# A two-layer graph network with expert layers on one core: the second attention's maximum by TensorE, a shorter choice of experts, and the first edges' terms loaded earlier

## The chip, the cores and the metric

The kernel runs on one core of a Trainium2 chip. The metric is the device time in microseconds of one execution: the median of several runs, lower is better. The core's engines are TensorE (PE, with PEld for its weight loads), VectorE (DVE), ScalarE (ACT), GpSimd (POOL) and SyncE (SP, which issues most DMAs). A matmul on 32-bit floats shows in the profile as two passes.

## What is computed

3125 nodes with 256 features, 100000 edges sorted by their target. Four residual steps, each on a normalized copy of `x`:

```python
x = x + gat(layernorm(x), edges, ...)          # two attention layers, 4 heads and 1 head
x = x + ffn0(layernorm(x))                     # 8 experts, two chosen once for all rows
x = x + gcn(layernorm(x), edges, ...)          # a linear layer, two graph convolutions
x = x + ffn1(layernorm(x))                     # 8 experts, two chosen for each row
```

Attention over the edges into a node (with a loop at each node) is

```python
e = leaky_relu(al_s[src] + al_d[dst], 0.2)
alpha = exp(e - segment_max(e, dst)) / segment_sum(...)     # for each target node
out = segment_sum(h[src] * alpha, dst)
```

and the first expert layer chooses its two experts from the mean row:

```python
routing = softmax(mean(x, axis=rows) @ Wr + br)
load = routing * N
scale = where(load > capacity, capacity / load, 1)          # capacity = ceil(N * 1.25 / 8)
routing = softmax(routing * scale);  top 2, softmax over the two, weights for both experts
out = layernorm(sum of the two weighted experts + x)
```

## The kernel before

Rows lie in 25 blocks of 128 nodes, in five groups of five. The stages follow each other on one core, each with work of the next one slipped in as "spare" tasks.

**Edges and the first attention layer** (0 to 990 us, `FirstLayer`). A counting pipeline (`count_step`, 391 chunks of 256 edges) makes a dense matrix of edge counts by one-hot matmuls (L1778). The first three blocks of nodes are computed densely from it. The other nodes go edge by edge: 258 chunks in 65 batches of four. For each batch POOL gathers the rows of the sources (L1918, eight indirect DMAs, a ring of three batches), SP loads `edge_turn` (the targets' places, L1933) and four small `window`s (the targets' terms, 14 to 20 rows of 16 bytes, L1937, each at an address that SP reads into a register at L1584). DVE makes one-hots of `edge_turn` (`place_turn`, L1951), PE picks the terms by them (`pick_terms`, L1964), DVE and ACT make the weights (L1973, L1980, L1985), DVE spreads them (L1991), PE multiplies (L2005), DVE adds to `agg` (L2018). The self loops of a piece of nodes are put into `agg` by `new_sums`: SP loads `loop_x` and `by_node` (L2064, L2066), DVE multiplies (L2075).

In `run`, ahead of the loop, the order written is: `open_sums`, eight gathers, the tasks of `new_sums(0)` each followed by a counting step, then the windows of batches 0 and 1 (L2387 to L2389), then `place_turn(0)`, `pick_terms(0)`, and so on. The framework schedules each engine's instructions by priority and readiness as it models them; priority is the order written. In the parts before and inside the loop `in_order` fixes the order on PE, DVE and ACT as written (before it on SP too); between them it does not.

**End of the first layer, second product** (990 to 1084). `norm_terms` makes scale and shift on small tiles (its Sqrt is L918), ACT applies them with Relu (L931), PE multiplies by W2 (L937), DVE sums the two attention terms of each block into the last two columns of `h2` (L943), ACT copies `h2` (L945).

**Second attention** (1084 to 1386). `sd` is copied from `h2` (L987). `attention_columns` takes maximum and minimum of the source terms on DVE (L784, L786) and over the partitions by a reduction on POOL (L790), makes three sets of columns (L802) and the flag for a range over 60. `attend_all` then runs 125 steps. For each group it transposes the target column (L829) and makes the two halves of `ab` on ACT (L831); each step has z on DVE (L840), Exp on ACT (L842), the product with the counts on DVE (L848) and ten PE passes into `po` (L857). Spare tasks ahead of the others are `degrees` (L947) and the nine arithmetic checks on the chunks' ranges (`check_tasks`, L1492), whose result decides at the very end whether a slow general version runs again.

**First expert layer** (1386 to 1634). The spare tasks of the last group normalize it, transpose it (L1232, L1233) and sum it over its nodes (L1237). `choose` makes the mean, the logits (L1263), two softmaxes with the load correction between them (L1266 to L1279), ranks, the experts' numbers (L1292), loads W1 and W2 of both (L1298, L1301), picks their bias (L1308), makes the two shares and scales W2 by them (L1322), and makes the mixed second bias (L1330 to L1335). POOL adds it to `xa` and beta to `x` (L1356, L1357). The loop over 13 chunks of nodes has W1 (L1384), Gelu into `hid` (L1387), W2 (L1394) and the sum (L1397). The pool `route` with `choose`'s small tiles is closed before `hid` is allocated, so `hid` may lie on the same memory, and a tile's first write waits for the last reader of what lay there.

**Convolutions and second expert layer** (1634 to the end). Two layers of dense products with the counts (L1100), with the routing of the second expert layer as spare tasks, then slots of 256 rows through their experts (L2877, L2887) and scattered sums (L2892).

Of the kernel before, what the change touches and what calls it, by code (L numbers as in the profile page):

```python
# [764 lines left out]
class Fast(Kernel):  # L765
# [13 lines left out]
    def attention_columns(self, sd, n, pool, doubt):  # L779


        nc = self.nc
        ends = pool.tile([P, 2, n], F32, name="ends")
        nc.vector.tensor_reduce(ends[:, 0, :], sd[:, :, :n].rearrange("p b k -> p k b"), AX.X,  # L784
                                ALU.max)
        nc.vector.tensor_reduce(ends[:, 1, :], sd[:, :, :n].rearrange("p b k -> p k b"), AX.X,  # L786
                                ALU.min)
        nc.vector.tensor_scalar(ends[:, 1, :], ends[:, 1, :], -1.0, None, op0=ALU.mult)
        top = pool.tile([P, 2, n], F32, name="ends_all")
        nc.gpsimd.partition_all_reduce(top.rearrange("p a k -> p (a k)"),  # L790
                                       ends.rearrange("p a k -> p (a k)"), P,
                                       bass_isa.ReduceOp.max)
        gap = pool.tile([1, n], F32, name="gap")
        nc.vector.tensor_add(gap, top[0:1, 0, :], top[0:1, 1, :])
        nc.vector.tensor_scalar(gap, gap, 60.0, None, op0=ALU.is_le)
        nc.vector.tensor_reduce(doubt, gap, AX.X, ALU.min)
        nc.vector.tensor_scalar(doubt, doubt, -1.0, 1.0, op0=ALU.mult, op1=ALU.add)
        cols = pool.tile([P, n, 3, NB], F32, name="att_cols")
        for k in range(n):
            for i, (x, op, f) in enumerate(((k, ALU.subtract, 0.2), (k, ALU.subtract, 0.8),  # L800
                                            (n + k, ALU.add, 0.8))):
                nc.vector.tensor_scalar(cols[:, k, i, :], sd[:, :, x], top[:, 0, k:k + 1], f,  # L802
                                        op0=op, op1=ALU.mult)
        return cols

    def attend_all(self, units, work, psum_out, aux, spare, loose=()):
# [7 lines left out]
        rows, cnts, zs, ws, pos = {}, {}, {}, {}, {}  # L814

        def lead(t):
# [6 lines left out]
            if j == 0:  # L823
                ab = work.tile([P, 2, GW], F32, name="ab", bufs=2)
                for b0, n in ((0, 3), (3, 2)):
# [39 lines left out]
        for t in range(n):  # L865
# [10 lines left out]
            if j == NB - 1:  # L876
                for i in range(GB):
                    units[u][2](g, i, pos[i])
# [310 lines left out]
class SharedExperts:  # L1189
# [147 lines left out]
    def run(self, onward, keep):  # L1337
# [4 lines left out]
        with ExitStack() as ctx:  # L1342
# [34 lines left out]
            for c0 in range(0, NP, n):  # L1377
                c1 = min(c0 + n, NP)
                hid = work.tile([P, 8, n], F32, name="hid")
                for r in range(2):  # L1380
                    for f in range(4):
# [7 lines left out]
                        if f % 2:  # L1389
                            go_on(1)  # L1390
# [1620 lines left out]
```

## Time and profile before

| What | us |
|---|---|
| median of three runs | 2423.31 (2422.38 to 2425.56) |
| the profiled execution, its own time | 2423.23 |
| its span in the profile | 2421.4 |
| PE busy in the span | 2110.2 (87%) |
| PEld, DVE, ACT, POOL busy | 1753.4, 1295.4, 1192.5, 738.0 |
| last L937 ends, first L857 starts | 1084.13, 1102.90 |
| last L857 ends, first L1384, first L1394 | 1385.79, 1418.01, 1428.96 |

A row of the order of time has start, duration, engine, line, operation, output and inputs by their names, shapes, and a count of instructions that were merged. In brackets stands the idle time of the engine ahead of it and what ended it; "remote" is a semaphore that the profile can't name, "issue" is time in which nothing that the profile shows was waited for. Times in the text that no row shows (a DMA's landing, one instruction of a merged row) are from the same execution's records. The granted clock of PE is either full (1.0) or half (0.5) at any time.

### The profile page before, as it was taken

How to read it: one execution, taken by the hardware profiler on the slowest of the kernel's cores; microseconds unless marked ns; L12 is line 12 of the kernel's file. 1: busy time of each engine (PE TensorE's matmuls, PEld its weight loads, DVE VectorE, ACT ScalarE, POOL GpSimd, SP SyncE). 2: the span in 40 equal slices, each digit the busy share in tenths (PEclk: the TensorE clock that was granted, in tenths of full speed). 3: DMA queues.
4: the chain of work that ended last, by engine and by line, in shares of the span. 5: the costliest groups of instructions: out<-in, count | busy, mean ns of one | idle time of the engine just before them, and what ended most of it. 6: DMA issues, size and time to landing. Idle time of an engine off the chain costs nothing. (4 is left out here: it accounts for less than half of the span.)

```text
span 2421.4 us, 35452 instructions
## 1 busy us (share of the span) xinstructions
PE 2110.2 (87%) x10573; PEld 1753.4 (72%) x10573; DVE 1295.4 (53%) x4225; ACT 1192.5 (49%) x2785; POOL 738.0 (30%) x749
## 2 busy tenths in 40 slices
PE   5477688797988888898999969999999998999997
PEld 5366566575666666777888758887887777888886
DVE  7667556575666666327888844334335765112221
ACT  3267666666777765623445425445434444222221
POOL 1666466666566771200000050000000323222221
PEclk9977899999999988898999979999999999999998
DMA  7433455465465665896222010003324546666773
GB/s 230 136 99 97 125 158 151 134 188 163 139 182 177 206 183 164 285 332 217 68 71 80 28 39 1 1 23 114 123 82 152 198 149 216 185 179 204 233 203 80
DMA packets 232172, 350.84 MB, mean 145 GB/s; under 512 B 38358, under 2 KB 175305, under 8 KB 228257
## 3 DMA queue, kind: packets, MB, share of 16 engines
q1 hardware_dynamic: 193697, 261.00, 33.4%
q0 software_dynamic: 36608, 86.14, 13.8%
q8 instruction: 88, 1.44, 0.2%
q10 hardware_dynamic: 1664, 1.31, 0.2%
q14 instruction: 115, 0.94, 0.1%
HBM read 262.68 MB, written 86.19 MB: 144 GB/s over the span
## 5 line engine op out<-in xcount | busy, mean ns | idle before, releaser
L1918 POOL DMA_INDIRECT edge_rows<-table,pick x516 | 524.3, 1016 | 318.3 <-PE edge_sums L2005 120.1
L2005 PE MATMUL edge_sums<-edge_moves,edge_rows 128*128 128x120 f32 x2064 | 319.0, 303 | 15.5 <-issue 9.0
L2005 PEld LDWEIGHTS edge_sums<-edge_moves,edge_rows 128*128 128x128 f32 x2064 | 298.8, 216 | 44.2 <-issue 14.0
L1100 PE MATMUL po<-parts,cnt_r 128*128 128x512 f32 x1250 | 312.0, 402 | 4.3 <-ACT cnt_r L1094 2.6
L1778 PE MATMUL ps<-hot_key,hot_lo 128*128 128x350 f16 (+2 forms) x782 | 203.3, 355 | 104.2 <-DVE acc L1808 28.3
L1800 ACT CAST acc<-ps 128x325 f32 (+2 forms) x391 | 179.2, 458 | 222.1 <-PE ps L1778 64.2
L857 PE MATMUL po<-h,w 128*128 128x257 f32 x1250 | 276.7, 382 | 3.3 <-ACT o L1006 2.3
L1100 PEld LDWEIGHTS po<-parts,cnt_r 128*128 128x128 f32 x1250 | 232.3, 189 | 54.9 <-ACT cnt_r L1094 3.4
L857 PEld LDWEIGHTS po<-h,w 128*128 128x128 f32 x1250 | 236.8, 191 | 38.9 <-ACT o L1006 3.9
L2879 ACT ACTIVATE hid<-ph,ffn_b 128x256 f32<-128x256 f32 (+1 forms) x232 | 105.9, 457 | 273.6 <-PE ph L2877 253.3
L1764 ACT ACTIVATE hot_lo<-iota_key,lo 128x128 f16<-128x128 f16 x662 | 229.0, 398 | 0.0
L1758 DVE TENSOR_SCALAR hot_key<-iota_key,key 128x350 f16<-128x350 f16 (+2 forms) x782 | 225.7, 326 | 1.2 <-issue 1.2
L2877 PE MATMUL ph<-xe,ffn_w 128*128 128x256 f32 (+1 forms) x928 | 195.4, 366 | 10.0 <-DVE o L1115 5.9
L1778 PEld LDWEIGHTS <-hot_lo 128*128 128x128 f16 x782 | 81.2, 110 | 155.9 <-issue 92.0
L2887 PE MATMUL py<-ffn_w,hid 128*128 128x256 f32 x848 | 190.1, 382 | 0.0
L2877 PEld LDWEIGHTS ph<-xe,ffn_w 128*128 128x128 f32 x928 | 163.7, 193 | 33.7 <-remote 6.3
L2887 PEld LDWEIGHTS py<-ffn_w,hid 128*128 128x128 f32 x848 | 160.5, 192 | 20.9
L2892 POOL DMA_INDIRECT out<-y,to x53 | 82.7, 1560 | 305.0 <-DVE y L2891 161.2
L842 ACT ACTIVATE z<-z,att_cols 128x640 f32<-128x640 f32 x125 | 103.2, 830 | 145.3 <-DVE z L840 121.1
L2018 DVE TENSOR_TENSOR agg<-agg,edge_sums 128x180 f32 (+1 forms) x258 | 80.3, 311 | 161.8 <-PE edge_sums L2005 49.3
L2251 PE MATMUL po<-x_rows,w 128*128 128x256 f32 x600 | 156.9, 398 | 5.6 <-issue 3.7
L1808 DVE TENSOR_TENSOR acc<-acc,ps 128x25 f32 x391 | 101.4, 259 | 87.1 <-ACT acc L1800 44.2
(448 smaller groups left out, 3235.6 us busy)
## 6 DMA issues: line engine op xcount, KB each, us to landing
ffn_w<-in_L_ffn_W SPq DMA_DIRECT2D x58, 1024.0 KB
cnt_h<-cnt SPq DMA_DIRECT2D x50, 800.0 KB
rows<-blank SPq DMA_DIRECT2D x109, 258.0 KB
cnt<-cnt SPq DMA_DIRECT2D x25, 800.0 KB
cnt<-acc SPq DMA_DIRECT2D x45, 400.0 KB
first_out<-first SPq DMA_DIRECT2D x56, 192.0 KB
normed<-first_out SPq DMA_DIRECT2D x16, 640.0 KB
cnt<-cnt SPq DMA_DIRECT2D x20, 480.0 KB
```

What stands on the lines that cost most here:

```text
L857: nc.tensor.matmul(pos[i][:, :D + 1], lhsT=w[:, ts(i, P)], rhs=moving[:, j, :D + 1], start=(j == 0), stop=(j == NB - 1))
L1100: nc.tensor.matmul(pos[b], lhsT=c[:, j - j0, ts(b, P)], rhs=parts[i][:, j].rearrange("p a m -> p (a m)"), start=(j == 0), stop=(j == NB - 1))
L1758: nc.vector.tensor_scalar(h[:, u, :NB * w], self.wide[:, :NB * w], self.key[:, t:t + 1], None, op0=ALU.is_equal)
L1764: nc.scalar.activation(l[:, u, :], self.wide[:, :P], AF.Abs, bias=self.lo[:, t:t + 1], scale=-1.0)
L1778: last = self.nc.tensor.matmul(ps[:, :n], lhsT=l[:, u, :], rhs=h[:, u, :n], start=(u == 0), stop=(u == CT - 1))
L1800: ins = self.nc.scalar.copy(self.acc[g][:, :, ds(o + 1, width(c) - 1)], self.parts[c][:, :, 1:])
L1918: return self.nc.gpsimd.indirect_dma_start(out=self.ring[:, e % (RB * BT), :], out_offset=None, in_=self.table, in_offset=bass.IndirectOff ...
L2005: nc.tensor.matmul(ps[:, f * 4 * w:f * 4 * w + EW], lhsT=self.rows_of(m)[:, e, ts(f, P)], rhs=self.spread[m % 2][:, e * 5 * w:e * 5 * w + EW],
L2251: self.nc.tensor.matmul(self.pos[i], lhsT=w[:, ts(i, P)], rhs=self.k.x[:, j, :], start=(j == 0 and i % 2 == 0), stop=(j == NB - 1), skip_g ...
L2877: nc.tensor.matmul(ph, lhsT=w1[:, c, ts(f, P)], rhs=xe[:, c, :], start=(c == 0), stop=(c == 1))
L2879: nc.scalar.activation(hid[:, f, :], ph, AF.Gelu, bias=b1[:, f:f + 1])
L2887: nc.tensor.matmul(py, lhsT=hid[:, f, ts(i, P)], rhs=w2[:, f, :], start=(f == 0), stop=(f == NF - 1))
```

## The change

Five things are changed.

1. The windows of batch 0 are written ahead of the first gathers and of `new_sums(0)`; those of batch 1 stay where they were.
2. `attention_columns` becomes `attention_top`: DVE's maximum, a transpose on PE, DVE's maximum along the row, and two matmuls with a row of +1 and of -1 that put the maximum and its negative on all partitions. Two sets of columns instead of three; the third goes into the bias of the Relus that make `ab`, and Exp's scale becomes -0.8. For the first group the target columns are transposed ahead (`spread_ends`), and one half of `ab` is made on DVE. The sums of L943 go straight into `sd`. The minimum and the flag become spare tasks (`range_tasks`), `degrees` becomes several small tasks behind eight empty ones.
3. `norm_terms` issues one Exp (with scale 0) behind its Sqrt.
4. `check_tasks` move from the second attention to the second convolution layer.
5. The first expert layer: the last group's sums are taken block by block behind each transpose. The correction `where(load > capacity, ...)` is a minimum of the routing with capacity / N; the division by N is folded into the bias's addition; ranks are taken from these values, and the second softmax is made behind the loads of the weights. The experts' numbers are picked in one instruction each. The mixed bias takes one matmul (`second_bias`), called behind the first four hidden tiles of the first chunk, and POOL's adds to `xa` and `x` follow it; those to `x` also wait for the scaled W2. `route` stays open, so `hid` lies elsewhere.

```diff
-    def attention_columns(self, sd, n, pool, doubt):
...
+    def attention_top(self, sd, signs, pool, psum):
+        nc = self.nc
+        ends = pool.tile([P, 2], F32, name="ends")
+        nc.vector.tensor_reduce(ends[:, 0:1], sd[:, :, 0], AX.X, ALU.max)
+        ps = psum.tile([P, 512], F32, name="po")
+        nc.tensor.transpose(ps[:1, :P], ends[:, 0:1], self.ident)
+        most = pool.tile([1, 1], F32, name="ends_most")
+        nc.vector.tensor_reduce(most, ps[:1, :P], AX.X, ALU.max)
+        for i in range(2):
+            nc.tensor.matmul(ps[:, P + i:P + i + 1], lhsT=signs[:, i, :], rhs=most, start=True,
+                             stop=True)
+        top = pool.tile([P, 2], F32, name="top")
+        nc.vector.tensor_copy(top, ps[:, P:P + 2])
+        cols = pool.tile([P, 2, NB], F32, name="att_cols")
+        for i, f in ((1, 1.0), (0, 0.2)):
+            nc.vector.tensor_scalar(cols[:, i, :], sd[:, :, 0], top[:, 0:1], f, op0=ALU.subtract,
+                                    op1=ALU.mult)
+        return cols, top, ends, most
...
+                top = units[u][1]
+                for b0, n, pt in units[u][2] if t == 0 else spread(units[u][3], g):
+                    part = lambda i: ab[:, i, b0 * P:(b0 + n) * P].rearrange(
+                        "p (i n) -> p i n", n=P)
+                    nc.scalar.activation(part(0), pt[:, :n, :], AF.Relu, bias=top[:, 1:2],
+                                         scale=-1.0)
+                    if t == 0:
+                        nc.vector.tensor_scalar(part(1), pt[:, :n, :], top[:, 0:1], 0.0,
+                                                op0=ALU.add, op1=ALU.max)
+                    else:
+                        nc.scalar.activation(part(1), pt[:, :n, :], AF.Relu, bias=top[:, 0:1])
...
         nc.scalar.activation(rstd, diff, AF.Sqrt, bias=self.eps)
+        nc.scalar.activation(t[0:1, 5, 0:1], diff[0:1, 0:1], AF.Exp, scale=0.0)
...
-            spare = deque([lambda: self.degrees(first, work, aux)] + first.check_tasks(work))
+            wait = lambda: None
+            spare = deque([wait] * 8 + self.degree_tasks(first, work, aux)
+                          + self.range_tasks(sd, ends, most, work, aux, self.doubt[:, 3:4]))
+            self.checks = first.check_tasks
...
+            spare.extend(self.checks(work))
             layer(1, work, finish1)
...
+        def turn_last(b):
+            turn(b)
+            n0 = (g * GB + b) * P
+            add_up(g + b, n0, n0 + P)
...
-        nc.vector.tensor_add(rw[:, 0, :], pl, br)
-        k.softmax8(rw, rw, route, "sm0", 1)
...
-        nc.vector.tensor_mul(rw, rw, load)
-        k.softmax8(rw, rw, route, "sm1", 1)
+        nc.vector.scalar_tensor_tensor(rw[:, 0, :], pl, 1.0 / N, br, op0=ALU.mult, op1=ALU.add)
+        top = route.tile([P, 1], F32, name="sm0_top")
+        nc.vector.tensor_reduce(top, rw, AX.X, ALU.max)
+        nc.vector.tensor_scalar(rw[:, 0, :], rw[:, 0, :], top, None, op0=ALU.subtract)
+        nc.scalar.activation(rw, rw, AF.Exp)
+        total = route.tile([P, 1], F32, name="sm0_total")
+        nc.vector.tensor_reduce(total, rw, AX.X, ALU.add)
+        nc.vector.reciprocal(total, total)
+        nc.vector.tensor_scalar(rw[:, 0, :], rw[:, 0, :], total, cap / N, op0=ALU.mult,
+                                op1=ALU.min)
...
+        k.softmax8(rw, rw, route, "sm1", 1)
...
+        for r in range(2):
+            self.scaled = nc.vector.tensor_scalar(self.w2[:, r], self.w2[:, r], tw[:, r:r + 1],
+                                                  None, op0=ALU.mult)
+        return own, b2
+
+    def second_bias(self, own, b2, ps_y):
+        k, nc = self.k, self.nc
+        pb = ps_y.tile([P, D], F32, name="py")
+        nc.tensor.matmul(pb, lhsT=own.to_broadcast([8, P]), rhs=b2, start=True, stop=True)
         nc.scalar.copy(self.b2, pb)
+        for b in range(NB):
+            nc.gpsimd.tensor_add(self.xa[:, b, :], self.xa[:, b, :], self.b2)
+            late = nc.gpsimd.tensor_add(k.x[:, b, :], k.x[:, b, :], self.beta)
+            self.tc.add_manual_dep(late.ins, self.scaled.ins.name, SYNC)
...
+                    if c0 == 0 and r == 0:
+                        self.second_bias(*shares, ps_y)
...
             self.open_sums(ctx, w1, stats)
+            for c in range(self.size[0]):
+                self.window(0, c)
             for e in range(BT):
                 self.gather(e)
...
-            for m in range(2):
-                for c in range(self.size[m]):
-                    self.window(m, c)
+            for c in range(self.size[1]):
+                self.window(1, c)
```

## The prediction

> **What bounds the kernel now.** I read the busy times by stage first, then the matmul queue's pauses, then the order of time inside each pause. The chain of waits is of no use here: it names only the last scatter. In the stages view the columns after each window are its length, the busy time of PE, PEld, DVE, ACT and POOL with counts, the granted clock and the DMA share.
>
> ```profile
> core 0: us, PE busy (x) PEld busy (x) DVE busy (x) ACT busy (x) POOL busy (x), PEclk, DMA share, GB/s
> 73.70:80.20 6.50, 0.00 (x0) 0.00 (x0) 2.50 (x11) 0.35 (x1) 4.90 (x5) 1.00 0.38 104
> 80.20:1084.10 1003.90, 819.42 (x4512) 656.41 (x4512) 602.14 (x2251) 638.15 (x1815) 541.08 (x551) 0.90 0.57 171
> 1084.10:1102.90 18.80, 3.10 (x14) 2.05 (x13) 12.58 (x74) 6.02 (x13) 0.52 (x2) 0.64 0.94 312
> 1102.90:1385.80 282.90, 280.58 (x1305) 244.08 (x1305) 237.32 (x389) 131.62 (x190) 0.24 (x2) 0.99 0.26 83
> 1385.80:1429.00 43.20, 16.09 (x54) 11.49 (x55) 26.01 (x88) 11.79 (x24) 28.10 (x41) 0.60 0.18 56
> 1429.00:1826.00 397.00, 391.09 (x1790) 324.62 (x1788) 148.37 (x418) 179.90 (x318) 8.61 (x19) 1.00 0.17 57
> ```
>
> PE is busy nearly all the time from 1102.9 to 1385.8 and from 1429 on. Between, it stands still three times: 6.5 us before the first edges, 18.8 us ahead of the second attention layer, 43.2 us around the choice of experts (16.1 us of work in it). Behind each pause comes work that PE sets the pace of (or, in the edge loop, queues that feed each other in a fixed order), so a pause cut by x us should move all that follows by x.
>
> **1. Terms of the first edges.** PE's own order of time, then DVE's (start, duration, engine, line, groups; in brackets the idle time and who ended it):
>
> ```profile
> 80.28 1.03 PE L1964 MATMUL edge_sums<-window,edge_turn 128*128 128x16 f32 x4 [6.59 <-remote]
> 83.11 0.35 DVE L1951 TENSOR_SCALAR edge_turn<-edge_turn,part_place 128x256 f32<-128x256 f32 x1 [4.53 <-DMA edge_turn<-places]
> ```
>
> SP issued the four window DMAs of batch 0 between 68.1 and 81.1, its register instructions between them taking 0.70 us each where they take 0.03 elsewhere, and only then (81.84) the second edge_turn. The change issues edge_turn 0, the register load (1.50) and four windows (0.45 each at SP's undisturbed pace of 90 us) when SP is free, from about 61 us: they are in by 66. What is moved behind them is SP's three pairs of loop_x and by_node, whose issue costs the same 1.2 us a pair. They go later by 1.8 us (if edge_turn and the register load fit SP's idle 59.05 to 61.09) to 3.9. The first by_node had landed 0.5 us before L2075 took it at 67.3, so that DVE line slips 1.3 to 3.4 us, and with it L1951 (74.59 before), which PE's L1964 needs: 76 to 78 instead of 80.28. The next late thing is DVE's second L1951 at 83.11, whose load now goes out near 72.5 and lands by 75; the rows of gathers 0 to 7 landed at 74.8. So L1973 comes at 79 to 80.5 instead of 83.51. POOL's gathers do not wait for SP. I take **-3.5 us**; bounds -6.6 (the whole pause) and +3 (the loads 3.4 late and SP slow all the same). 64 batches follow in the same source order, which should carry this to 990.
>
> **2. Exp's table ahead (norm_terms).** One Exp behind the Sqrt makes ACT load a table there. The first Sqrt load in the trace takes 1.28 and ACT idled 0.88 for DVE's chain, 993.15 to 994.02; load and activation (1.28 + 0.2) end at 994.67: **+0.65** on the first L931, which PE waits for. Bounds 0 (if it is put behind the first Relus) and +1.5. The gain, no load at 1098.9, is in the next sum.
>
> In the trace an activation starts 0.01 us behind its load's end (1098.90 + 1.28, then 1100.19). The Trainium skill ("ScalarE: Activation LUTs", What ACT_TABLE_LOAD costs) puts a drain of about 1.38 us behind each load; by it, as an estimate, this edit would cost about 2.0 instead of 0.65. The trace disagrees, and I stay with it.
>
> **3. The maximum by TensorE.**
>
> ```profile
> 1085.59 0.15 DVE L788 TENSOR_SCALAR ends<-ends 128x1 f32<-128x1 f32 x1
> ...
> 1094.89 0.37 POOL L790 PARTITION_ALL_REDUCE ends_all<-ends  x1 [9.56 <-DMA deg_cols<-deg_row]
> ...
> 1096.05 1.33 PE L829 MATMUL aux<-ident,att_cols 128*128 128x128 f32 x5 [11.91 <-DVE att_cols L802]
> ...
> 1098.90 1.28 ACT L842 ACT_TABLE_LOAD   x1
> 1102.90 13.48 PE L857 MATMUL po<-h,w 128*128 128x257 f32 x53 [1.02 <-DVE w L848]
> ```
>
> From the ends (1085.74) to the reduced row 9.15 us pass on POOL, then transposes, ab, z, table load, exp, w. The new chain from L943's last sum at 1084.95: max 0.18 (L784); transpose into a bank that L945 has just left at 1085.35, 0.44 to its reader (L958); reduce 0.28 (L960); two matmuls with one row, four passes like L1263, 1.05; copy 0.16: 1087.4. On DVE two columns (0.2 each) and the two halves of ab, 0.46 and 0.35: 1088.6. On ACT the other halves, 0.75; but there the gcn weights' six DMA issues (L1051 to L1059) run from 1085.04 to 1088.36 and will stand ahead: 1089.15. Then z 0.87, exp 0.83, w 0.82 with small gaps: PE at 1091.75 instead of 1102.90. The transposes of b (1.33 before) hide under the wait. Counts, needed at 1090.9, landed at 1089.0. The check arithmetic on DVE (1085.9 to 1102) is gone from here; degrees and the range test come as spare tasks beside a PE that is 99% busy. dinv's Sqrt (L1061), done in the pause before, will then cost two table loads in the loop; such a pair at 1340.65 left PE running. **-11.2 us**; bounds -12.5 (ACT's issues not ahead: -11.7, and a faster start) and -9 (K=1 matmuls and DVE's order worse than the rows).
>
> **4. The short choice.**
>
> ```profile
> 1398.88 0.65 DVE L1270 TENSOR_SCALAR load<-rw 128x8 f32<-128x8 f32 x1
> ...
> 1409.77 0.64 DVE L1288 SCALAR_TENSOR_TENSOR scr<-hot,expert 128x8 f32<-128x8 f32 x1
> ...
> 1410.45 0.63 DVE L1292 TENSOR_SCALAR number<-eid 1x2 int32<-1x2 f32 x1
> 1411.01 0.15 DVE L1308 SCALAR_TENSOR_TENSOR scr<-small,hot 128x8 f32<-128x8 f32 x1
> ...
> 1418.01 5.49 PE L1384 MATMUL ph<-xa_t,ffn_w 128*128 128x256 f32 x12 [0.46 <-ACT ffn_b_sum L1335]
> ...
> 1422.71 1.28 ACT L1387 ACT_TABLE_LOAD   x1 [4.75 <-DVE ffn_w L1322]
> ```
>
> DVE's eight-element instructions take 0.65 while POOL adds beta (1396.74 to 1413.79) and 0.15 to 0.23 otherwise or with a PSUM source. The change takes the load correction and the second softmax off the chain, and POOL's adds behind it. From ACT's last copy at 1394.03: the last block's sum 0.2 (2x106 elements; 1.33 for 2x1130), mean 0.16, PE 1.06: DVE at 1395.6 (1396.91 before). Seven steps at 0.16 to 0.26 with gaps: 1.6. Ranks, five at 0.19 to 0.26: 1.15. Two picks 0.45, number 0.14: 1398.95 instead of 1411.08. SP issues 0.70 later, and the first w1 landed 3.53 us after its issue: PE at 1403.2. It now waits for no bias, and the hidden tile no longer lies on `route`, so Gelu need not wait for the scaled w2 (4.75 before). PE: 12 passes at the half clock's 0.427, 20 at 0.216 and the bias's two: 9.9 us, so L1394 starts at 1413.1 instead of 1428.96. w2, landed 6.5 and 7.3 after issue, is scaled by 1409.9, in time; Gelu starts near 1405 at 0.47 each, faster than PE delivers. POOL's 50 adds (0.7 each) now run 1410 to 1445 beside PE; L1397 takes block b at about 1416.7 + 6.9b, POOL has it at 1410.7 + 1.4b. **-15.8 us**; bounds -17.3 and -12.1 (only the chain's part).
>
> **5. Checks moved** into the second convolution layer: about 9 us of DVE in small pieces where PE is bound and DVE is idle half the time, one more SP issue (0.25). At the seam of the layers (1816 to 1827), where PE, ACT and DVE hand on in turn, a few may be in the way: **+0.5**, bounds 0 and +2.5.
>
> Sum: -3.5 + 0.65 - 11.2 - 15.8 + 0.5 = -29.35. The profiled execution took 2423.23 us (span 2421.4), the runs' median is 2423.31, so 2423.2 - 29.3 = **2394 us**.
>
> **Rivals.**
> - The first edges gain nothing: the self loops' loads come late on a DVE that works in order, and SP stays slow. For it: L2075's loads had 0.5 us to spare. Against: PE and DVE stood 6.6 and 4.5 us for just these transfers. 2394 + 3.5 to 6.5 = 2399. Chance 0.20.
> - The choice doesn't do all it says: Gelu still ends up behind the scaled w2. Then only 12.1 of 15.8 comes: 2398. For it: the wait of 4.75 is on a tile reused in memory, and the new layout may lay `hid` on another late tile. Chance 0.12.
> - The clock stays full in the shortened pauses. Before, it was half from 1389.7 to 1423.8 and for 17.1 us from 1089.3; the first eight full-size passes behind the pause took 0.427 instead of 0.216. Both starts would gain about 1.7 and 2.6: 2390. Against: the pause of 3.15 us at 2044.5 already brought 3.4 us of half clock. Chance 0.08. The Trainium skill ("TensorE: Matmul & The Clock Gate", Part 1, and Part 4 on PE-mode transposes) says that an idle window of some 3.4 us is enough, and that transposes don't count as busy; by it the clock falls here too, as I forecast.
> - Slower: the edge loop's pace. In its static order each of 64 batches (13.3 us apart) waits for its edge_turn or rows; if windows now meet the loads of loops in SP's queue in every batch, as SP did at 92.75 to 103.9, each loses time. From 29.3/64 = 0.46 us a batch it eats all gains; at 1 us the time is 2394 + 64 = 2458. Against: source order inside the loop is unchanged. Chance of slower 0.06; of just cancelling 0.03.
> - The forecast: 0.51.
>
> The forecast alone reaches from 2388 to 2401. With the first two rivals and the unknown bounds I give 2386 to 2407. A measurement here tells 0.2% (about 5 us). Faster 0.91, same 0.03, slower 0.06.
>
> **What would show it.** PE's L1964 near 77 and L1973 near 80; the last edge sums some 3.5 us earlier; no POOL reduce at L790's place and L857's first matmul some 8 us behind the last L937; number 5 us behind the last xa_t copy, DVE at 0.2 there, L1394 some 19 us behind it; every later stage as long as before. I am wrong if the stage from the first batch to 990 changes its length by over 3 us, if SP's windows are still slow, or if Gelu again waits for ffn_w.

## The result, and the profile after

| | before | after |
|---|---|---|
| median of five runs, us | 2423.31 (2419.06 to 2429.86) | 2403.42 (2402.05 to 2410.10) |
| profiled execution, its span | 2423.23, 2421.4 | 2402.05, 2400.3 |

The ratio is 0.992, with a 95% interval of 0.990 to 0.9939: 20 us faster, where 29 were forecast. Stage by stage, from the records of the two profiled executions (the text's differences are made of these):

| Stage | before | after | difference |
|---|---|---|---|
| start to the first edge multiplication | 87.43 | 87.65 | +0.22 |
| from there to the last edge sums | 872.58 | 872.37 | -0.21 |
| to the end of the second product | 124.12 | 123.72 | -0.40 |
| to the first weighted multiplication of the second attention | 18.76 | 7.27 | -11.49 |
| second attention's loop on PE | 282.89 | 284.08 | +1.19 |
| to the last copy of xa_t | 8.25 | 8.25 | 0.00 |
| choice and first experts, to the first convolution multiplication | 243.93 | 228.71 | -15.22 |
| convolutions and second experts, to the last W1 multiplication | 762.59 | 767.68 | **+5.09** |
| sum | 2400.55 | 2379.73 | -20.82 |

The stages view after, in windows that answer to those of before (length; busy PE, PEld, DVE, ACT, POOL with counts; granted clock, DMA share, GB/s):

```profile
core 0: us, PE busy (x) PEld busy (x) DVE busy (x) ACT busy (x) POOL busy (x), PEclk, DMA share, GB/s
73.70:82.00 8.30, 0.49 (x2) 0.10 (x1) 2.90 (x6) 0.35 (x1) 3.90 (x5) 1.00 0.68 198
82.00:1083.80 1001.80, 806.79 (x4514) 648.96 (x4515) 600.42 (x2256) 640.63 (x1817) 538.45 (x554) 0.91 0.58 172
1083.80:1091.00 7.20, 1.33 (x10) 0.84 (x8) 5.43 (x17) 2.94 (x5) 0.47 (x3) 0.81 0.88 309
1091.00:1375.10 284.10, 281.74 (x1313) 244.83 (x1313) 237.42 (x391) 136.38 (x196) 0.00 (x0) 0.99 0.30 96
1375.10:1403.00 27.90, 15.33 (x52) 11.69 (x53) 15.46 (x84) 11.74 (x23) 9.11 (x12) 0.63 0.29 85
1403.00:1800.30 397.30, 391.39 (x1791) 324.70 (x1789) 149.28 (x426) 179.27 (x317) 27.63 (x47) 1.00 0.17 57
1800.30:1812.00 11.70, 9.40 (x29) 7.46 (x30) 8.93 (x50) 4.72 (x5) 0.00 (x0) 0.71 0.42 140
```

The pause of 18.8 us ahead of the attention is 7.2, the stretch around the choice is 27.9 instead of 43.2. The pause ahead of the first edges is still there, and 8.3 us long. The last row is new: a stretch at the seam of the two convolution layers with a mean granted clock of 0.71.

**The first edges after** (PE's and DVE's order of time):

```profile
79.14 1.23 DVE L2137 TENSOR_TENSOR agg<-loop_x,by_node 128x1024 f32<-128x1024 f32 x1 [2.54 <-issue]
80.58 0.25 DVE L1823 TENSOR_SCALAR hot_lo<-iota_key,lo 128x128 f16<-128x128 f16 x1 [0.20 <-issue]
81.30 1.23 DVE L2137 TENSOR_TENSOR agg<-loop_x,by_node 128x1024 f32<-128x1024 f32 x1 [0.47 <-issue]
...
82.07 1.04 PE L2026 MATMUL edge_sums<-window,edge_turn 128*128 128x16 f32 x4 [5.40 <-DVE hot_lo L1823]
...
83.14 0.19 DVE L2035 TENSOR_TENSOR edge_p<-edge_sums,edge_rows 128x32 f32<-128x32 f32 x1
```

L2026 is the old L1964, L2035 the old L1973. All four windows were on their way by 70.1. But the first pick starts at 82.07, later than before (80.28): its row names DVE's `hot_lo` (L1823, a step of the counting) as what ended the wait, and DVE has the first of the self loops' products (L2137) ahead of that. These products come at 79.14 and 81.30 instead of 67.30 and 68.75, since their rows were issued only from 73.2 on.

**The maximum and the choice after**:

```profile
1084.48 0.17 DVE L785 TENSOR_REDUCE ends<-sd 128x1 f32<-128x25 f32 x1
...
1085.02 0.27 PE L787 MATMUL po<-ident,ends 128*1 128x128 f32 x1 [0.73 <-ACT h L978]
...
1086.38 0.16 DVE L794 COPY top<-po 128x2 f32<-128x2 f32 x1 [0.76 <-PE po L791]
...
1089.22 0.83 ACT L872 ACTIVATE z<-z,att_cols 128x640 f32<-128x640 f32 x1 [1.63 <-DVE z L870]
...
1091.05 3.34 PE L887 MATMUL po<-h,w 128*128 128x257 f32 x7 [4.70 <-DVE w L878]
```

```profile
1386.25 0.23 DVE L1332 TENSOR_SCALAR rw<-rw,sm_total 128x8 f32<-128x8 f32 x1
...
1388.12 0.16 DVE L1345 TENSOR_SCALAR number<-eid 1x2 int32<-1x2 f32 x1
...
1392.21 1.19 PE L1393 MATMUL py<-ffn_b,own_share 8*128 8x256 f32 x2 [6.45 <-issue]
1393.33 9.90 PE L1444 MATMUL ph<-xa_t,ffn_w 128*128 128x256 f32 x32
1403.07 7.07 PE L1456 MATMUL py<-ffn_w,hid 128*128 128x256 f32 x32
```

From the column's maximum (1084.65) to the copy of the result (1086.54) 1.9 us pass, where 9.5 passed by POOL (1085.74 to 1095.26). DVE's eight-element steps take 0.16 to 0.23 down to the number, which is ready 4.94 us behind the last copy of xa_t (17.05 before).

**The seam of the convolution layers after** (ACT and PE), where the five microseconds begin to go:

```profile
1800.39 0.48 ACT L1122 ACTIVATE split<-aux,dinv 128x256 f32<-128x256 f32 x1 [0.79 <-PE aux L1119]
1800.76 1.78 ACT L1143 CAST cnt_r<-cnt_h 128x1920 fp32r<-128x1920 f16 x1
...
1802.60 9.69 PE L1149 MATMUL po<-parts,cnt_r 128*128 128x512 f32 x29 [2.31 <-ACT cnt_r L1143]
```

The same place before:

```profile
1825.43 1.79 ACT L1094 CAST cnt_r<-cnt_h 128x1920 fp32r<-128x1920 f16 x1
1827.13 0.47 ACT L1073 ACTIVATE split<-aux,dinv 128x256 f32<-128x256 f32 x1
...
1827.27 12.99 PE L1100 MATMUL po<-parts,cnt_r 128*128 128x512 f32 x56 [1.06 <-ACT cnt_r L1094]
```

The second layer's first multiplication waits for the counts' cast, which now stands in ACT's order behind the last block's `split` (before, ahead of it), and 2.31 us pass instead of 1.06. In the clock's records it is half from 1801.6, within that pause, to 1808.5; before, it stayed full there.

### The profile page after: what moved, and what is told of

It is laid out like the page before. It is cut to its first block, busy times and chain, and to the rows that moved or that the text cites. A ratio compares the mean times of both kernels' runs of the same rounds, so it can differ in the third digit from the quotient of the medians.

```text
span 2400.3 us, 35484 instructions
## 1 busy us (share of the span) xinstructions
PE 2100.4 (88%) x10578; PEld 1746.8 (73%) x10578; DVE 1282.4 (53%) x4222; ACT 1196.3 (50%) x2785; POOL 734.5 (31%) x751
## 5 line engine op out<-in xcount | busy, mean ns | idle before, releaser
L2067 PE MATMUL edge_sums<-edge_moves,edge_rows 128*128 128x120 f32 x2064 | 313.3, 299 | 13.1 <-issue 10.2
L1149 PE MATMUL po<-parts,cnt_r 128*128 128x512 f32 x1250 | 319.5, 409 | 5.0 <-ACT cnt_r L1143 3.8
L2067 PEld LDWEIGHTS edge_sums<-edge_moves,edge_rows 128*128 128x128 f32 x2064 | 293.1, 212 | 42.2 <-issue 17.9
L1840 PE MATMUL ps<-hot_key,hot_lo 128*128 128x350 f16 (+2 forms) x782 | 198.0, 346 | 117.7 <-DVE acc L1870 41.4
L1149 PEld LDWEIGHTS po<-parts,cnt_r 128*128 128x128 f32 x1250 | 235.2, 191 | 60.0 <-ACT cnt_r L1143 4.6
L1826 ACT ACTIVATE hot_lo<-iota_key,lo 128x128 f16<-128x128 f16 x662 | 227.6, 395 | 0.0
L2940 PE MATMUL ph<-xe,ffn_w 128*128 128x256 f32 (+1 forms) x928 | 195.0, 366 | 11.2 <-DVE o L1164 6.2
L2950 PEld LDWEIGHTS py<-ffn_w,hid 128*128 128x128 f32 x848 | 159.1, 190 | 20.5
```

Of the source, the lines that this page charges most:

```text
L1149: nc.tensor.matmul(pos[b], lhsT=c[:, j - j0, ts(b, P)], rhs=parts[i][:, j].rearrange("p a m -> p (a m)"), start=(j == 0), stop=(j == NB - 1))
L1826: nc.scalar.activation(l[:, u, :], self.wide[:, :P], AF.Abs, bias=self.lo[:, t:t + 1], scale=-1.0)
L1840: last = self.nc.tensor.matmul(ps[:, :n], lhsT=l[:, u, :], rhs=h[:, u, :n], start=(u == 0), stop=(u == CT - 1))
L2067: nc.tensor.matmul(ps[:, f * 4 * w:f * 4 * w + EW], lhsT=self.rows_of(m)[:, e, ts(f, P)], rhs=self.spread[m % 2][:, e * 5 * w:e * 5 * w + EW],
L2940: nc.tensor.matmul(ph, lhsT=w1[:, c, ts(f, P)], rhs=xe[:, c, :], start=(c == 0), stop=(c == 1))
L2950: nc.tensor.matmul(py, lhsT=hid[:, f, ts(i, P)], rhs=w2[:, f, :], start=(f == 0), stop=(f == NF - 1))
```

## Experiments

Twelve runs on three more chips, four on each. On all three the kernel before takes about 2275 us instead of 2423 (the last section comes to that). So each run is compared with a run of the changed kernel on its chip, or by stage lengths that hardly differ between chips; on the first of the three, with the runs on the tests and the first two on part 1, there is no run of the changed kernel.

**The kernels themselves.** 

> The changed kernel itself, unaltered, beside the others on one chip: the measure for all runs that differ from it by one edit. Both theories of each edit expect it 0.8% under the kernel before, as on the first chip; where the chip runs the edge loop faster, the microseconds and not the share should stay: 18 to 22 us.

> The kernel before, unaltered, for its stage lengths on the same chip as the others. If SP's and DVE's instructions take their normal time here ahead of the first batch, the waits of 6.5 us that part 1 was to shorten are shorter from the start; if they take 0.7 us until the gathers' rows are in, the first multiplication is at 87 as in the first profile.

> The changed kernel itself once more, as the measure for the three others on this chip. On the two chips so far it stood 0.8 and 1.1% under the kernel before; 0.7 to 1.2% here.

Measured: after_again 0.9893 of the kernel before (0.9869 to 0.9918; 2257.38 us), before_again 1.0008, after_third on the fourth chip 0.9917 (0.9901 to 0.9932; 2256.08). The gain stays as microseconds: 17 and 21.5. Stage lengths of the kernels with the changed order of the tests: from first convolution to last W1 753.7 to 757.6 (most 754.5) against 748.19 before; the edge loop, 743.7 to 756.1, scatters over 12 us from execution to execution and hides small edits in it. In before_again the first edge multiplication is at 78.09, in after_again at 79.19: here too part 1 gains nothing.

**Where did five microseconds go: the tests at the seam.** In one run the nine index tests are written behind the first group of the second layer, in the other among the attention's tasks:

```diff
-            spare.extend(self.checks(work))
             layer(1, work, finish1)
...
                 if b % GB == GB - 1:
                     spare.extend(router.tasks(b - GB + 1, GB, out))
+                if b == GB - 1:
+                    spare.extend(self.checks(work))
```

> The changed kernel with the first layer's nine index tests (the moved work of part 5) put behind the first group of the second convolution layer instead of ahead of it. Theory 'seam': the tests only hurt because their DVE pieces push the casts of the first counts behind them, which makes TensorE's pause between the two layers 2.31 us instead of 1.06 and lets the clock fall to half for 6.8 us right after it. Then the pause is 1.06 again, the clock stays full at the seam, the stretch from the first matmul of layer 0 to the last slot's end is some 4 us shorter than the changed kernel's 767.7 us (763 to 764.5), and the time is 2398 to 2400. Rival 'the work itself': nine tests cost their DVE time wherever they stand in this layer; then the stretch stays at 767 to 768 and the time within 2 us of the changed kernel's 2403. Second rival 'the clock falls anyway': pause 1.06 but still half clock behind it; stretch about 766.5.

> The changed kernel with the same nine index tests back among the spare tasks of the second attention loop, where they stood before the change, behind the degree and range tasks. Theory 'seam': the seam of the convolution layers is as before (pause 1.06, full clock), the stretch from layer 0 to the last slot 763 to 764.5 instead of 767.7; the attention loop, whose TensorE is 99% busy and whose DVE has 40 of 283 us free, keeps its 284.0 us within 0.5; time 2398 to 2400. Rival: the tests delay the weights of that loop, which gets 1 to 5 us longer, and the gain at the seam is lost: 2400 to 2404.

Measured: 0.9889 (0.9868 to 0.991; 2248.76 us) and 0.9899 (0.988 to 0.9918). The stretch is 748.16 and 750.15, some 6 and 4 us less; the times themselves don't stand clear of the changed kernel's on the other chips (0.9893 and 0.9917). The attention's loop keeps its 284.2, with a pause of 7.93 instead of 7.27 ahead of it in the second run. With the tests written behind the first group, ACT and PE at the seam:

```profile
1663.42 1.79 ACT L1143 CAST cnt_r<-cnt_h 128x1920 fp32r<-128x1920 f16 x1
1665.12 0.47 ACT L1122 ACTIVATE split<-aux,dinv 128x256 f32<-128x256 f32 x1
...
1665.26 7.09 PE L1149 MATMUL po<-parts,cnt_r 128*128 128x512 f32 x23 [1.05 <-ACT cnt_r L1143]
```

The cast is ahead of the split again, the pause 1.05. The tests don't run behind the first group, though: DVE takes them at 1667.0 to 1678.4, from 1.8 us behind the layer's first multiplication on, where in the changed kernel they begin 5 us ahead of it (1797.6). So the move took them out of the handover and not into the middle of the layer. There they cost nothing measurable, so it isn't their work.

Divided on these chips: the pause +1.25 (12.12 instead of 10.87 from the last multiplication of one layer to the first of the next, in every run), and the second layer itself, 175.1 to 176.7 with the tests at the seam, 170.7 in both with them written behind the first group, 171.0 before, 172.9 with the tests in the attention. Its time at half clock is 16 us in seven of the eight kernels with the tests at the seam, instead of 10.2 before and with the tests written behind the first group. That is worth some 3 of these 5: 6.8 us instead of 3.4 at its start, and 10.2 instead of 6.8 in a second stretch some 127 us on. That second one is 10.2 with the tests in the attention too, so it isn't shown to come from the seam.

The rest, some 2.4 us, is in the passes of PE. Two views at full clock, from 10.7 us into the layer on, with the tests written behind the first group and in after_third:

```profile
1676.00:1792.00 116.00, 113.60 (x553) 92.91 (x552) 82.40 (x343) 53.45 (x77) 25.43 (x25) 1.00 0.54 172
```

```profile
1687.10:1804.00 116.90, 115.32 (x542) 92.08 (x541) 79.30 (x320) 53.08 (x76) 23.37 (x24) 1.00 0.52 169
```

PE is busy for 1.7 us longer with 11 instructions fewer. In the records, passes of L1149 that follow each other within 0.26 us do so after 0.2334 us on average in all nine profiles with the tests at the seam, after 0.2274 in the five others; in the first layer it is 0.233 in all fourteen. That lasts to the layer's end, while the tests end 10 us into it. What the edit also moves is memory: at the seam the tests' tiles are the first that the layer's pool takes, ahead of `cnt_h` and `cnt_r`. That this is the cause is not shown. On the first chip the division is another: +1.24 at the pause, +5.68 in the layer, -1.84 behind it, with 27.3 us of half clock from the seam on instead of 23.9.

"The clock stays full" was wrong in part: here half a clock of 3.4 us follows even the pause of 1.05, in all four profiles on these chips, and of 6.8 most pauses of 2.31.

**Why did part 1 gain nothing.** Three runs: part 1 undone; only eight gathers ahead of the first batch; and both batches' terms first, self loops last.

```diff
-            for c in range(self.size[0]):
-                self.window(0, c)
             for e in range(BT):
                 self.gather(e)
...
-            for c in range(self.size[1]):
-                self.window(1, c)
+            for m in range(2):
+                for c in range(self.size[m]):
+                    self.window(m, c)
```

> The changed kernel with part 1 alone undone: the four terms of the first batch are loaded behind the self loops' rows and the gathers again. Theory A (part 1 moved the wait without shortening it: the first pick stood behind DVE's self-loop products, whose rows now came later, while SP, DVE and TensorE all got an instruction only every 0.7 us until the gathers' rows were in): first batch's multiplication at 87.4 to 87.8 and the last edge sums at 960 as in both kernels; time within 1.5 us of the changed kernel. Theory B (the forecast's: part 1 gains 3.5 us, but something else of the change ate it, for example the other code layout): the first multiplication goes to 90 to 91 and the time rises by 3 to 4 us.

```diff
                 self.count_step(i)
-                self.gather_behind(i - 2)
...
             self.spread_edges(0)
+            for _ in range(BT):             # held until the weights are spread
+                self.gather(self.first_rows.popleft())
```

> The changed kernel with the gathers of the second batch's rows (numbers 8 to 15) held until the first batch's weights are spread, so that 8 instead of 15 gathers run ahead of the first batch. Theory A1 (all engines get their instructions slowly, one per 0.7 us, for as long as the burst of gathers has rows in flight): the slow stretch ends near 72 to 73 instead of 82, the first pick is at 74 to 77 instead of 82.07, the first multiplication at 78 to 82 instead of 87.65; if the edge loop then keeps its pace, its end comes 4 to 7 us earlier than 960 (time 2396 to 2399); if the second batch's rows come too late, part of it is given back. Rival A2 (the slow stretch has another cause, such as the windows' own loads or code loading): SP's and DVE's instructions still take 0.7 us until about 82, first multiplication 86 to 89, time within 2 us.

```diff
-            for c in range(self.size[0]):
-                self.window(0, c)
+            for m in range(2):
+                for c in range(self.size[m]):
+                    self.window(m, c)
...
             self.spread_edges(0)
+            for task in own:                # new_sums(0)
+                task()
```

> The changed kernel with the terms of both first batches ahead on SP's queue and the self loops' rows and products behind the first batch's spread weights. Theory A (part 1 gained nothing because DVE, in its fixed order, took the later self-loop rows ahead of the first sum, and TensorE the second batch's pick ahead of the first multiplication): first pick at 69, first sum at 73 to 74.5, first multiplication at 75 to 76.5 instead of 79.2. Rival (the gathers' rows set the first sum): the first multiplication stays at 78 to 80. The end of the edge loop is expected to follow by at most these 3 us, within its own scatter of some 6 us from run to run.

Measured: first_windows_back 0.9925 (0.9904 to 0.9946), first multiplication at 77.31; that is 1.9 us earlier than with part 1 in after_again, and the time can't be told from the changed kernel's on the other chips. second_rows_later 0.9952 (0.9937 to 0.9968), first multiplication 78.70. It could not decide between its theories: on this chip no instruction takes 0.7 us to begin with, so the slow stretch that it was to shorten wasn't there; by its share of the kernel before, holding the rows back costs a little against the changed kernel on the other chips (0.9893 and 0.9917), and gains nothing. What holds the first batch up is plain in after_again (PE and DVE):

```profile
69.16 1.03 PE L2026 MATMUL edge_sums<-window,edge_turn 128*128 128x16 f32 x4 [0.51 <-DVE edge_turn L2013]
...
70.40 1.23 DVE L2137 TENSOR_TENSOR agg<-loop_x,by_node 128x1024 f32<-128x1024 f32 x1 [1.01 <-DMA by_node<-loops]
...
73.37 1.23 DVE L2137 TENSOR_TENSOR agg<-loop_x,by_node 128x1024 f32<-128x1024 f32 x1 [1.54 <-DMA by_node<-loops]
...
76.36 0.41 DVE L2013 TENSOR_SCALAR edge_turn<-edge_turn,part_place 128x256 f32<-128x256 f32 x1 [1.43 <-DMA edge_turn<-places]
76.76 0.19 DVE L2035 TENSOR_TENSOR edge_p<-edge_sums,edge_rows 128x32 f32<-128x32 f32 x1
...
78.31 1.01 PE L2026 MATMUL edge_sums<-window,edge_turn 128*128 128x16 f32 x4 [7.78 <-DMA window<-terms]
```

The first pick starts at 69.16, six microseconds earlier than in before_again (75.47). Its result then waits: DVE takes two self-loop products, each behind its late rows, and the second batch's `edge_turn` before the first sum (76.76; before_again 76.55); and PE takes the second batch's pick, whose windows stand in SP's queue behind a self-loop load, before the first multiplication. With the self loops last (sums_behind):

```profile
68.74 1.04 PE L2026 MATMUL edge_sums<-window,edge_turn 128*128 128x16 f32 x4 [0.41 <-DVE edge_turn L2013]
...
74.01 0.19 DVE L2035 TENSOR_TENSOR edge_p<-edge_sums,edge_rows 128x32 f32<-128x32 f32 x1 [4.24 <-DMA edge_rows<-table,pick]
...
75.68 2.03 PE L2067 MATMUL edge_sums<-edge_moves,edge_rows 128*128 128x120 f32 x8 [0.38 <-issue]
```

The multiplication is at 75.64, 3.7 us earlier, as its theory said, and what ends last is now the gathers' rows. The time doesn't follow: 0.9935 (0.9918 to 0.9953), 2259.74 us against 2256.08 for after_third. The edge loop's scatter is larger than the 3.7 us, so what a head start there is worth is not settled.

**What in part 3 made the gain: POOL's reduction?**

```diff
-        nc.tensor.transpose(ps[:1, :P], ends[:, 0:1], self.ident)
...
+        nc.gpsimd.partition_all_reduce(every, ends[:, 0:1], P, bass_isa.ReduceOp.max)
```

> The changed kernel with the attention's maximum over the partitions made by POOL's reduction again (one column instead of two; the transpose, the reduction of the row and the two one-row multiplications of part 3 are gone, two small DVE steps make the two signs), everything else of part 3 kept. Theory 'POOL is slow' (the forecast's: from the ends to the reduced row 9.15 us passed on POOL, 1.9 us now by TensorE): the first weighted multiplication comes 13 to 15 us behind the second product's end instead of 7.3, time +6 to +8. Rival 'the queue' (the 9 us were mostly waits for the degree's load and the tests around it, which part 3 also moved away): 7 to 9 us behind, time within 2 us.

Measured: 0.9957 (0.994 to 0.9973), 2264.35 us, +8.3. First weighted multiplication 18.64 us behind the second product: the whole gain of this pause is gone, though the tests and the degree's chain are out of the way.

```profile
950.47 0.17 DVE L785 TENSOR_REDUCE ends<-sd 128x1 f32<-128x25 f32 x1
...
961.75 0.38 POOL L787 PARTITION_ALL_REDUCE ends_all<-ends  x1 [10.54 <-issue]
```

The reduction is 0.38 us in its row, and 11.5 us pass from its input (950.64) to its result (962.13). Part of it comes back: the loop that follows takes 282.29 instead of 284.4 in after_third. So a loop that starts 11 us earlier loses 2.1 of them again, as in the changed kernel (+1.19). PE isn't idle for longer in it: 2.3 us in all kernels, and nothing in its first 45 us. Eight small passes, the transposes for the degrees, the range and the second group, run within the long pause, and in the loop where the pause is short: the stages views count 1305 PE instructions before and 1313 after, and the loop loses some 0.6 us by them at each of two places. The loop also has 4.8 us of half clock in after_third instead of 2.7, worth 1.0.

**What in part 4: the chain, or beta's additions moved out of its way?**

```diff
-            late = nc.gpsimd.tensor_add(k.x[:, b, :], k.x[:, b, :], self.beta)
-            self.tc.add_manual_dep(late.ins, self.scaled.ins.name, SYNC)
...
                 shares = self.choose(route, psum)
+                for b in range(NB):
+                    nc.gpsimd.tensor_add(k.x[:, b, :], k.x[:, b, :], self.beta)
```

> The changed kernel with the 25 additions of beta on POOL free to run as soon as beta has landed, some 3.8 us behind its issue and so from about 2.8 us behind the last copy of xa_t, instead of behind the scaled w2. Theory 'shared' (an eight-element DVE instruction takes 0.65 us beside POOL's additions and 0.15 to 0.24 without them, so moving them was part of the gain of part 4): the last dozen steps to the expert's number take 0.65 each, the number comes 9 to 11 us behind the last copy instead of 4.94, TensorE's first multiplication of the experts 4 to 6 us later, time +4 to +6. Rival (the short chain alone made the gain): number 4.9 to 5.2 behind, time within 1.5 us of the changed kernel.

Measured: 0.9943 (0.9922 to 0.9964), 2266.8 us against 2257.38 for after_again. The number is 8.29 us behind the last copy (9 to 11 expected), and the stretch to the first convolution 235.6 instead of 227.6 to 228.9 in the other kernels with the short choice (243.0 in before_again): 7 to 8 of the 14 to 15.5 us that part 4 gains hang on the moved additions. (Of the 9.4 us in time some 3 more lie in the convolutions, 757.6 instead of 754.5; why isn't known.)

```profile
1252.90 0.16 DVE L1331 RECIPROCAL sm_total<-sm_total 128x1 f32<-128x1 f32 x1
1252.91 17.34 POOL L1417 TENSOR_TENSOR x_rows<-x_rows,beta 128x256 f32<-128x256 f32 x24 [300.81 <-DVE sm_total L1330]
1253.10 0.55 DVE L1332 TENSOR_SCALAR rw<-rw,sm_total 128x8 f32<-128x8 f32 x1
...
1254.31 0.76 DVE L449 TENSOR_TENSOR rk_eq<-rw 128x64 f32<-128x64 f32 x1
1254.99 0.15 DVE L429 TENSOR_REDUCE sm_top<-rw 128x1 f32<-128x8 f32 x1
...
1257.92 0.56 DVE L1345 TENSOR_SCALAR number<-eid 1x2 int32<-1x2 f32 x1
...
1266.08 1.19 PE L1393 MATMUL py<-ffn_b,own_share 8*128 8x256 f32 x2 [13.46 <-issue]
```

L1332 takes 0.23 in the changed kernel and 0.55 here, beside the additions. My time for it was too low (+4 to +6), because the shares behind the number are slowed as well, and PE's first work, the second bias, waits for them (1266.08); W1, issued at 1259.26, does not set it (in the changed kernel PE takes it 4.3 us behind its issue).

**The early Exp.**

```diff
-        nc.scalar.activation(t[0:1, 5, 0:1], diff[0:1, 0:1], AF.Exp, scale=0.0)
```

> The changed kernel without the early exponential of part 2 (one element, its value unused), so that the table for the attention's exponential is loaded when it is first needed. Theory 'covered' (ACT stands idle between the halves of ab and the first exponential for 1.6 us, so the load of 1.28 hides there): the first weighted multiplication comes 0 to 0.5 us later behind the second product, and the stage ahead of it gets at most 0.7 shorter; time within 1 us. Rival (the forecast's): the load stands in the way for 1.28 us at the exponential and saves 0.65 before: +0.6 us in all, first multiplication 8.3 to 8.6 us behind the second product instead of 7.3.

Measured: 0.9898 (0.9877 to 0.9919). From the first layer's last output to L937's first pass 4.10 us instead of 4.64 (-0.54); from the second product to the first weighted multiplication 7.70 instead of 7.27 (+0.43). The two cancel: the load of 1.28 is nearly covered at either place.

**A version from the findings**: tests written behind the first group, part 1 undone.

> The changed kernel with the index tests behind the first group of the second convolution layer and with part 1 undone. If both findings hold, the stretch from layer 0 to the last slot is 748 to 750 instead of 754.3, the first multiplication of the edge loop at 77 to 78 instead of 79.2, and the time 6 to 9 us under the changed kernel's on this chip. Rival (the two gains do not add, or the loop's scatter hides them): within 3 us.

Measured: 0.9887 (0.9869 to 0.9904), 2247.19 us, 8.9 under after_third beside it (0.9901 to 0.9932; the two intervals meet only at their ends). The stretch is 749.83, 4.9 less than in after_third, the first multiplication at 76.37. The edge loop is 7 us shorter in the profiled executions, within its scatter, so how much of the 8.9 the edits made isn't settled. It stands no better than the tests' move alone (0.9889, on another chip): the gain of undoing part 1 on top isn't shown.

## Why the prediction was right, and where it was wrong

The sum, -29.35, was off by 8.5 us against the -20.82 of the stages: 3.5 in part 1, 4.6 in part 5, 0.9 in part 3 and 0.6 in part 4, less 1.05 where the stage ahead of the second product got 0.40 shorter and not 0.65 longer. The measured 2403.4 is outside of what the forecast alone was given (2388 to 2401) and inside the whole range, which was opened up to 2407 for the rivals and "the unknown bounds". Parts 2 to 4, nine tenths of the sum, came nearly as described.

- **Part 1, -3.5 forecast, none measured.** The first rival came true. The step that failed is "they go later by 1.8 us ... DVE line slips 1.3 to 3.4 us, and with it L1951". The self loops' rows were issued 11 to 15 us later on the first chip, since SP's slow stretch (0.70 and more each) began from the second window on, at 64, where it had begun at 67 before: in both kernels it sets in with the windows, and what starts it no run shows. And both DVE's order (products and the second `edge_turn` ahead of the first sum) and PE's (second pick ahead of the first multiplication) were waits that I had seen only half: I named the second L1951, and let its load land by 75, though it stood behind everything that I had moved ahead of it. On chips without the slow stretch the step fails all the same, by these orders.
- **Part 2, +0.65 forecast**, +0.54 measured by leaving it out, so the price was right. The gain on the other side was 0.43, not a whole load.
- **Part 3, -11.2 forecast.** The pause lost 11.49, with the first pass at 1091.05, 7.27 us behind the second product, where 7.6 was forecast; but the loop gave 1.19 back. Net -10.3. The mechanism was right, and max_by_pool shows that it is the reduction's stay on POOL at this place (why it is slow there is open, see the last section). What the loop gave back I had put at nothing: "degrees and the range test come as spare tasks beside a PE that is 99% busy". Their passes and the second group's transposes are eight more on PE in the loop, and the half clock there is 4.0 us instead of 3.5.
- **Part 4, -15.8 forecast, -15.22 measured.** Number 4.94 us behind the last copy (5 forecast), first L1456 19.7 (19), Gelu waits for PE only (0.33). PE started W1 0.8 us later than forecast, because the second bias stands ahead of it. I had the split of the gain right in kind: beta_at_once shows that 7 to 8 us of it is the additions' new place.
- **Part 5, +0.5 (0 to 2.5) forecast, +5.09 measured.** This term is the largest miss. I saw the place, "the seam of the layers (1816 to 1827), where PE, ACT and DVE hand on in turn", and priced only the tests' own pieces. The runs show their DVE work at nothing, a handover that turns round on ACT and DVE (+1.25), behind it a clock that falls for longer (3.4 us more, 1.7 us of time), and slower passes through the whole layer, which nothing in the forecast has. A pause's price has the clock in it: I counted that in the shortened pauses, and left it out where a pause grew. What the passes are slow from stays open.
- **The clock in the shortened pauses** fell as forecast: it is half from 1088.3 to 1095.1 and from 1378.4 to 1398.9. The rival by which it stays full is out. So is the slower rival: the edge loop kept its pace (872.37 against 872.58).

The Trainium skill ("TensorE: Matmul & The Clock Gate", Part 1) gives a free-running window of about 3.4 us, idle for which the clock falls. The half-clock stretches here are multiples of it (3.4, 6.8, 20.5). But here it fell behind pauses of 1.05 (in four of five profiles) and 2.31 (in all nine), shorter than a window. The 12 us ahead of the seam, with transposes, are busy by 6.9 of 12.3; Part 4 says that transposes don't count as busy in the same way, which would fit. No run here parts the two.

## What to carry to other kernels

- Loading something earlier moves its rivals later in the same queue. Follow every engine's fixed order from the moved load to the work that it is for: the gain is what is left when all other inputs of that work, and all that stands ahead of it in any order, have been looked up.
- Filler work belongs in a stage that one engine bounds, not at a handover where several engines pass work on in turn. Nine small tests cost nothing measurable 1.8 us behind the handover and some 6 us across it: 1.25 in the pause, up to 3 by the clock, and some 2.4 by passes that may be slow from where the tests' tiles lie. An edit that seems to move only work can move memory too: compare the time of single passes in the stages around it.
- Look at when moved work really runs. Tests written behind a layer's first group ran at its start.
- Small steps on DVE that lie on a path shouldn't run beside POOL's additions: half of the gain of a shorter chain was in moving these (7 to 8 of 14 to 15.5 us).

## What the runs showed of the hardware that was not expected

- **POOL beside DVE** stretches kinds of instruction, not all. Of steps on 8 to 64 elements, most TENSOR_SCALAR go from 0.23 to 0.55 or more and most TENSOR_TENSOR with both inputs in SBUF from 0.22 to between 0.64 and 0.76 (one, L451, keeps its 0.21), while TENSOR_REDUCE keeps its 0.15 and the steps with a PSUM input their 0.17. The Trainium skill ("SBUF — State Buffer", Who interferes with whom) says just this of the port pair that DVE and POOL share: reductions never contend. The rows agree.
- **POOL's reduction over partitions** stood 10.5 us in front of a row of 0.38, with nothing shown that it waited for. That isn't the price of the reduction itself. An earlier one of the same program, here in the kernel before, starts 0.14 us behind its input (54.68):

```profile
54.82 0.50 POOL L1663 PARTITION_ALL_REDUCE ends_all<-ends  x1 [27.94 <-DVE ends L1661]
```

  In the records POOL has an instruction MODIFY_POOL_CONFIG ahead of each reduction. For this one it stands at 26.9, 28 us ahead; in the second attention it comes only behind POOL's IOTAs, at 1085.56, 9.3 us ahead of the reduction, and at 951.45 in max_by_pool, 10.3 us ahead. So the time may belong to that instruction, and a kernel that has it earlier might keep the reduction; none was run. The Trainium skill ("GPSIMD Engine Reference", 2.1 Instruction dispatch) puts about 6 us, unseen in a profile, on the first call of freshly loaded code. That would be of this kind; no run here shows what the 10.5 are.
- **The same program is 6% slower on one chip**, in the edge loop above all: 872 us on the first chip in both kernels, 744 to 756 on the three others. The transfers' packets are alike there (a packet of the gathers' queue takes 164 ns in the median in both before and before_again). What differs is the engines' pace of instructions, as ahead of the first batch; SP's four windows, after on the first chip and after_again:

```profile
63.64 6.50 SPq L1999 DMA_DIRECT2D window<-terms  x4
```

```profile
63.49 1.98 SPq L1999 DMA_DIRECT2D window<-terms  x4
```

  The cause was not found; no run went back to that chip.
